# A write of an unread tile on GpSimd behind the transfers by index, in a four-layer attention and expert kernel

## The chip, the cores and the metric

The kernel runs on one core of one Trainium2 chip. The metric is the device time of one execution in microseconds; the time of a kernel is the median over its runs. Engines are named as in the profile: PE is TensorE's matmuls and PEld its weight loads, DVE is VectorE, ACT is ScalarE, POOL is GpSimd, SP is SyncE.

## What is computed

The input is `x`, 8 sequences of 256 tokens with 128 channels. Four layers follow, each added to its own input after a layer norm:

```python
x = x + _L0_attn_a_ref(_layernorm(x), w_qkv, w_proj, b_proj)     # grouped linear, 16 heads of 8
x = x + _L0_ffn_ref(_layernorm(x), router_w, router_b, w1, b1, w2, b2)
x = x + _L0_attn_b_ref(_layernorm(x), Wq, Wk, Wv, Wo, qn_w, kn_w)  # q and k normalised per head
x = x + _L0_ffn_ref(_layernorm(x), ...)                           # the same experts again
```

`_L0_ffn_ref` is a mixture of 16 experts. A softmax over `h @ router_w + router_b` gives each token a weight per expert; the four largest are kept and scaled to sum to one; the output is the weighted sum of `gelu(h @ w1[e] + b1[e]) @ w2[e] + b2[e]` over those four experts. The reference computes all experts for all tokens and multiplies by a weight that is zero for twelve of them.

## The kernel before

The kernel computes each token only in its four experts. Tokens lie 128 to a tile, 16 tiles in all, in `x_sb`; a sequence is two tiles, and the tiles fall into two halves of eight.

An expert layer `f` (0 or 1) works on a half `hf` in this way. For a group of two or four tiles the routing (`ln_route` to `rows_of`, on DVE and PE) finds for each token the rows in a DRAM buffer where copies of it go, one row in the block of each chosen expert, and puts them into `dst`. `send` (L1000) then writes the normalised rows `h` to `sent[hf]` by those indices: one transfer by index (L1007) for each tile and each of the four choices, issued by GpSimd. When all tiles of a half are sent, SyncE loads the rows of a pair of experts (`load`, L1069, into `xs`), PE transposes them (`turn`, L1085), and the two matmuls of each expert follow (`front`, L1102, and `second`, L1125); ACT's queue writes the results to `made[hf]`. `fetch` (L1254) brings them back by the indices in `src`: again one transfer by index (L1262) on GpSimd for each tile and each choice, into a tile `yg` with four buffers, or into `yg_last` for the last half of the last layer. `combine` (L1269) adds the four weighted rows to `x_sb` on DVE (L1273). The last two tiles of the last layer are not sent at all; they go through all experts in place (`all_experts`). So there are 120 sends and 120 fetches.

The first two choices of a token (`EARLY` is 2) avoid the last pair of experts, so their results can be fetched before that pair is done: `fetch` is called once for columns 0 and 1 and once for columns 2 and 3. For the first four tiles of a half, and for all six tiles of the last half, these are two separate calls:

```python
            for t in ts[:n]:
                at(end - 0.5, fetch, f, t, 0, EARLY, last)
            for t in ts[:n]:
                at(end + 1.5, fetch, f, t, EARLY, TOPK)
```

Besides the transfers by index, GpSimd sets up constants in the first 10 us, among them the four value tiles `vst` (L299: a write of 128 x 1088 f32 each), and in the first attention adds the projection's bias to `x_sb` (`add_bias`, L636; eight times). DVE adds the attention's output to the same rows later (L892).

The order of work on PE, ACT, DVE and SP is written out by hand: a list `plan` of steps with places, sorted and issued under a guard that names these four engines:

```python
    with tc.manual_schedule(engines={ET.PE, ET.Activation, ET.DVE, ET.SP}):
```

GpSimd is not named there. Its order is settled by the framework's planner when the program is built; the planner also puts in the semaphores.

Of the kernel before, what the change touches and what calls it, by code (L numbers as in the profile page):

```python
# [36 lines left out]
F32 = mybir.dt.float32  # L37
# [7 lines left out]
P = 128  # L45
# [67 lines left out]
def fast_path(  # L113
# [21 lines left out]
    nc = tc.nc  # L135
# [24 lines left out]
    def limits(cap):  # L160
        return [(E - 2) * cap] * EARLY + [E * cap] * (TOPK - EARLY)
# [6 lines left out]
    const = ctx.enter_context(tc.tile_pool(name="const", bufs=1))  # L168
# [38 lines left out]
    xf = x_in.rearrange("b n c -> (b n) c").rearrange("(t p) c -> p t c", p=P)  # L207
    of = out.rearrange("b n c -> (b n) c").rearrange("(t p) c -> p t c", p=P)
    x_sb = const.tile([P, NT, C], F32, name="x_sb")

    def load_x(b0, b1_):
        ts = slice(b0 * TB, b1_ * TB)
        nc.sync.dma_start(x_sb[:, ts, :], xf[:, ts, :])
# [104 lines left out]
    def after(ins, others):  # L318
        for o in others:
            tc.add_manual_dep(  # L320
                ins.ins,
                o.ins.name,
                mybir.DependencyInfo(mybir.DependencyClass.Sync, mybir.DependencyReason.DATA),
                reason="rows by index",
            )
# [414 lines left out]
    def needs(*what):  # L740
        assert done.issuperset(what), what
# [258 lines left out]
    def send(f, g):  # L1000

        hf = g.t0 // TPH
        needs(("rows", f, g.t0))
        before_all = list(loaded[hf] or cleared[hf])
        for i in range(g.n):
            for c in range(TOPK):
                ins = nc.gpsimd.indirect_dma_start(  # L1007
                    out=sent[hf],
                    out_offset=bass.IndirectOffsetOnAxis(
                        ap=dst[:, g.t0 + i, c : c + 1], axis=0  # L1010
                    ),
                    in_=g.h[:, i, :],
                    in_offset=None,
                )
                key = f"sent{f}{hf}"
                if scattered[hf]:
                    tc.declare_no_dep(ins.ins, group=key, reason="different rows")
                tc.add_to_no_dep_group(key, ins.ins)
                after(ins, before_all)
                scattered[hf].append(ins)  # L1020

    def plain_exp(g):
        t = work.tile([P, g.n, E], F32, tag=f"exl1{g.n}", name="ex1", bufs=1)
        nc.vector.tensor_scalar(t, g.ex, -1.0, 1.0, ALU.mult, ALU.add)
        nc.vector.reciprocal(t, t)
        nc.vector.scalar_tensor_tensor(g.ex, g.ex, 1.0, t, ALU.add, ALU.mult)
# [227 lines left out]
    def fetch(f, t, c0, c1, last=False):  # L1254

        needs(("fetchable", f, t))
        if last:
            yg[t] = many[:, t % TPH]
        elif c0 == 0:
            yg[t] = work.tile([P, TOPK, C], F32, tag="yg", name="yg", bufs=4)  # L1260
        for c in range(c0, c1):
            nc.gpsimd.indirect_dma_start(  # L1262
                out=yg[t][:, c, :],
                out_offset=None,
                in_=made[t // TPH][0 : limits(CAPS[f][t // TPH])[c]],
                in_offset=bass.IndirectOffsetOnAxis(ap=src[:, t, c : c + 1], axis=0),
            )

    def combine(t, k_next):  # L1269
        y = yg.pop(t)  # L1270
        x = x_sb[:, t, :]
        for c in range(TOPK):
            nc.vector.scalar_tensor_tensor(  # L1273
                x, y[:, c, :], wgt[:, t, c : c + 1], x, ALU.mult, ALU.add
            )
        if k_next is not None:
            ln_stats(k_next, t)
            done.add(("combined", t))
        else:
            nc.sync.dma_start(of[:, t, :], x)  # L1280
# [21 lines left out]
    def routed(f):  # L1302
        k = 2 * f + 1
        for hf in range(NH):
            earlier = []
            parts = ((0, 2), (2, 3), (3, 4)) if hf == 0 else ((0, 1), (1, 2), (2, 3), (3, 4))
            for (b0, b1_), places, fills in zip(
                parts, ROUTE[f][hf], FILL_ROUTE[f][hf], strict=True
            ):
                b0, b1_ = b0 + hf * SH, b1_ + hf * SH  # L1310
                g = Group(b0 * TB, b1_ * TB)
                g.all = (f, g.t1) == (1, NT)
                n = [base[2 * f] + b1_ * SEQ + p for p in places]
                before = list(earlier)
                at(n[0], ln_route, k, g, int(n[0]))
                at(n[1], ln_normalise, k, g, "r")
                at(n[2], ln_transpose, g, None, fills[0])
                at(n[3], route1, g)
                at(n[4], chosen, f, g)
                at(n[5], route2, g, before, in_attention(int(n[5])), fills[1])  # L1320
                if g.all:
                    at(n[7], weights_of_all, g)
                    whole.append(g)
                    continue
                at(n[6], rows_of, f, g)
                at(n[6], send, f, g)
                at(n[7], route3, f, g)
                earlier.append(g)
# [5 lines left out]
    def fetched(f, k_next):  # L1334
        k = 2 * f + 1
        for hf in range(NH):
            end = base[k] + (hf + 1) * E
            ts = [hf * TPH + i for i in range(SENT[f][hf])]
            last = k_next is None and hf == NH - 1
            n = len(ts) if last else 4  # L1340
# [4 lines that stand above are left out]
            for i, t in enumerate(ts):  # L1345
                m = COMBINE[f][hf]
                if i >= n:
                    at(end + m[i - 4], fetch, f, t, 0, TOPK)
                at(end + m[i], combine, t, k_next)
            if k_next is None:  # L1350
                continue
            for i, places in enumerate(PROJECT[hf]):
                g = gb[hf * SH + i]
                n = [end + p for p in places]
                at(n[0], to_heads, g, FILL_PROJECT[hf][i][0])
                at(n[1], project_b1, g)
                at(n[2], squares_b, k_next, g)
                at(n[3], project_b2, g, in_attention(int(n[3])))
                at(n[4], project_b3, g)
                at(n[5], project_b4, g, FILL_PROJECT[hf][i][1])  # L1360
                at(n[6], split, g, wn)
                at(n[7], stack_in, g)
# [635 lines left out]
def kernel(tc: tile.TileContext, *args):  # L1998
    nc = tc.nc
    with tc.tile_pool(name="flag", bufs=1) as pool:  # L2000
        flag = pool.tile([1, 1], I32, name="flag")
        fast_path(tc, flag, *args)
        n_bad = nc.values_load(flag[0:1, 0:1], min_val=0, max_val=6 * P)  # L2003
        with tc.If(n_bad > 0):
            general_path(tc, *args)
# [45 lines left out]
```

## Time and profile before

| what | value |
|---|---|
| median of 14 runs | 449.15 us (446.36 to 452.74) |
| the profiled execution | 451.16 us; span from first to last instruction 449.4 us |
| mean granted TensorE clock | 0.964 |
| busy: PE, ACT, DVE, POOL | 391.7, 281.0, 257.4, 245.3 us |
| sends (L1007) | 120, mean 966 ns, between 71.40 and 356.01 us |
| fetches (L1262) | 120, mean 951 and 961 ns, between 171.49 and 442.25 us |

Where the stages lie, by the timeline: the first attention runs to about 105 us, with the first half's sends from 71.4 to 111.8; the first expert layer from 116 to about 217 us, with its fetches from 171.5 to 211.5 and from 223.3 to 263.3; the second attention from about 217 to 315; its sends from 275.0 to 356.0; the second expert layer to the end, with its fetches from 372.2 to 442.3.

A line of a group reads: line of the kernel, engine, operation, output tile <- input tiles, shape, count, then busy time in us and mean ns of one, then the engine's idle time just before these instructions and what ended it. A line of a timeline reads: start and duration in us, engine, line, operation, tiles, count, and in brackets the idle time before it with what ended it; "issue" means that nothing which the profile shows was waited for.

### The profile page before, as it was taken

The numbers are of one execution on the slowest core, as the hardware profiler recorded it, in microseconds if no ns is written. First come the engines' busy times: TensorE is split into PE (matmuls) and PEld (weight loads), VectorE is DVE, ScalarE is ACT, GpSimd is POOL, SyncE is SP. The second block draws the span as 40 slices with busy tenths as digits, with TensorE's granted clock in tenths as the row PEclk, the third lists the DMA queues.
The fourth block names the chain that finished last, engine by engine and source line by source line (L and its number), as shares of the span: only waits on it lengthen the run. The fifth ranks groups of instructions, "written<-read, shape, count | busy, mean of one in ns | idle before, by whom it ended". The sixth has DMA issues, their size and how long they took to land. (4 is left out here: it accounts for less than half of the span.)

```text
span 449.4 us, 10606 instructions
## 1 busy us (share of the span) xinstructions
PE 391.7 (87%) x3884; PEld 254.1 (57%) x3884; DVE 257.4 (57%) x1037; ACT 281.0 (63%) x543; POOL 245.3 (55%) x292
## 2 busy tenths in 40 slices
PE   7999897983699999999979887888699997999991
PEld 3444553541476776766634344444477775777991
DVE  4544656564177511589648898876367413346464
ACT  4799987484453444465699988989464443553440
POOL 8110005777637725776077734777761506777772
PEclk9999998698699999999999999999699999999997
DMA  5234346751966455534434333341543334444222
GB/s 172 58 113 129 113 155 208 234 147 47 294 215 190 152 181 167 167 118 145 130 114 124 101 103 92 93 142 61 171 135 116 112 148 126 149 142 140 66 66 66
DMA packets 46668, 60.69 MB, mean 135 GB/s; under 512 B 8657, under 2 KB 28161, under 8 KB 46609
## 3 DMA queue, kind: packets, MB, share of 16 engines
q1 hardware_dynamic: 34000, 34.13, 25.4%
q0 software_dynamic: 7712, 15.81, 12.2%
q10 hardware_dynamic: 4896, 10.00, 5.8%
q8 instruction: 33, 0.54, 0.5%
q14 instruction: 27, 0.21, 0.2%
HBM read 31.86 MB, written 28.05 MB: 133 GB/s over the span
## 5 line engine op out<-in xcount | busy, mean ns | idle before, releaser
L1007 POOL DMA_INDIRECT sent<-h,dst x120 | 115.9, 966 | 79.1 <-issue 31.1
L1262 POOL DMA_INDIRECT yg<-made,src x96 | 91.3, 951 | 67.3 <-DMA made<-ys 27.2
L802 ACT ACTIVATE ex<-ps_st 128x1024 f32<-128x1024 f32 x120 | 116.1, 1027 | 14.2 <-PE ps_st L793 12.9
L1125 PE MATMUL ps_y<-w_sb,g 128*64 128x128 f32 x1216 | 80.5, 278 | 2.8 <-DVE ys L1132 2.7
L1125 PEld LDWEIGHTS ps_y<-w_sb,g 128*64 128x64 f32 x1216 | 65.1, 136 | 26.0 <-issue 11.6
L1110 ACT ACTIVATE g<-ps_h,b1T 128x320 f32<-128x320 f32 (+1 forms) x128 | 58.9, 511 | 33.1 <-PE ps_h L1102 29.7
L1102 PE MATMUL ps_h<-hs,w_sb 128*128 128x320 f32 (+1 forms) x256 | 78.9, 432 | 0.0
L1132 DVE TENSOR_TENSOR ys<-ps_y,b_bc 128x384 f32<-128x384 f32 (+1 forms) x64 | 30.3, 473 | 75.2 <-PE ps_y L1125 71.5
L823 PE MATMUL ps_av<-ex,vst 128*32 128x256 f32 x1024 | 70.5, 394 | 1.2 <-ACT av L833 0.9
L1086 ACT COPY hs<-pt_x 128x384 f32<-128x384 f32 (+1 forms) x64 | 26.1, 413 | 58.6 <-PE pt_x L1085 40.3
L1102 PEld LDWEIGHTS ps_h<-hs,w_sb 128*128 128x128 f32 x256 | 44.7, 195 | 10.3 <-issue 2.0
L793 PE MATMUL ps_st<-qst,kst 32*128 32x256 f16 x480 | 33.1, 274 | 12.2 <-ACT ex L802 7.8
L823 PEld LDWEIGHTS ps_av<-ex,vst 128*32 128x32 f32 x1024 | 27.2, 111 | 28.0 <-issue 13.6
L1085 PE MATMUL pt_x<-ident,xs 128*128 128x128 f32 x152 | 30.6, 303 | 14.1 <-DMA xs<-sent 14.1
L1273 DVE SCALAR_TENSOR_TENSOR x_sb<-yg,wgt,x_sb 128x128 f32<-128x128 f32 x96 | 33.7, 351 | 2.6
L1085 PEld LDWEIGHTS pt_x<-ident,xs 128*128 128x128 f32 x152 | 17.8, 150 | 22.0 <-issue 20.7
L636 POOL TENSOR_TENSOR x_sb<-x_sb,bp_bc 128x256 f32<-128x256 f32 x8 | 5.8, 729 | 42.5 <-DVE h L532 42.5
L793 PEld LDWEIGHTS <-kst 32*128 32x128 f16 x480 | 10.8, 92 | 30.8 <-issue 25.8
L1262 POOL DMA_INDIRECT yg_last<-made,src x24 | 23.1, 961 | 7.3 <-issue 7.0
L1198 ACT ACTIVATE g<-ps_h,b1T 128x256 f32<-128x256 f32 x32 | 13.4, 471 | 18.0 <-PE ps_h L1190 15.1
L892 DVE TENSOR_TENSOR x_sb<-pp,x_sb 128x256 f32<-128x256 f32 x16 | 6.7, 419 | 26.9 <-PE pt_h L546 15.5
L465 DVE BATCH_NORM_STATS2 st<-x_sb 128x6 f32<-128x128 f32 x64 | 17.9, 280 | 3.5 <-DMA x_sb<-in_L_attn_a_x_dram 2.4
(191 smaller groups left out, 528.7 us busy)
## 6 DMA issues: line engine op xcount, KB each, us to landing
xs<-sent SPq DMA_DIRECT2D x24, 320.0 KB
made<-ys ACTq DMA_DIRECT2D x24, 320.0 KB
sent<-zero SPq DMA_DIRECT2D x20, 256.0 KB
w_sb<-in_L_ffn_w_dram SPq DMA_DIRECT2D x16, 256.0 KB
qk_rows<-qk_parts SPq DMA_DIRECT2D x15, 256.0 KB
qst<-qk_rows SPq DMA_DIRECT2D x60, 64.0 KB
kst<-qk_rows SPq DMA_DIRECT2D x60, 64.0 KB
xs<-sent SPq DMA_DIRECT2D x8, 256.0 KB
```

The source lines that it names most:

```text
L793: nc.tensor.matmul(ps[:, hh, c * N : (c + 1) * N], kst[rows, f, c * P : (c + 1) * P], qst[rows, f, :], start=True, stop=True,)
L802: nc.scalar.activation(ex, ps.rearrange("p h (c n) -> p h c n", c=TB), AF.Exp, scale=SCALE / (UP * UP),)
L823: nc.tensor.matmul(acc[32 * i : 32 * i + 32, hf * N : (hf + 1) * N], groups[b].v[:, c, v0 : v0 + W], ex[i // 2][:, i % 2, m, :], start=(jj ...
L1007: ins = nc.gpsimd.indirect_dma_start(out=sent[hf], out_offset=bass.IndirectOffsetOnAxis(ap=dst[:, g.t0 + i, c : c + 1], axis=0), in_=g.h[: ...
L1085: nc.tensor.transpose(pt[:, (j - j0) * P : (j - j0 + 1) * P], x[:, j, :], ident)
L1086: nc.scalar.copy(hs[r][:, :, j0:j1, :], pt[:, : (j1 - j0) * P].rearrange("p (j a q) -> p a j q", a=2, q=HP),)
L1102: nc.tensor.matmul(ps[:, n, :cap], w1_sb[r][:, a, n * P : (n + 1) * P], hs[r][:, a, :RJ].rearrange("p j q -> p (j q)"), start=True, stop=True,
L1110: nc.scalar.activation(g[:, n, :RJ].rearrange("p j q -> p (j q)"), ps[:, n, :cap], AF.Gelu, bias=b1T[:, e * NI + n : e * NI + n + 1],)
L1125: nc.tensor.matmul(acc[a * HP : (a + 1) * HP, (j - j0) * C : (j - j0 + 1) * C], gs[2 * r + a][:, n, j, :], w2_sb[r][:, a, n, :], start=(n ...
L1132: nc.vector.tensor_tensor(ys[r][:, j0:j1, :], acc[:, : (j1 - j0) * C].rearrange("p (j c) -> p j c", c=C), b2_bc[:, r, :].unsqueeze(1).to_b ...
L1262: nc.gpsimd.indirect_dma_start(out=yg[t][:, c, :], out_offset=None, in_=made[t // TPH][0 : limits(CAPS[f][t // TPH])[c]], in_offset=bass.I ...
L1273: nc.vector.scalar_tensor_tensor(x, y[:, c, :], wgt[:, t, c : c + 1], x, ALU.mult, ALU.add)
```

## The change

A tile `rest_of` of 128 x 1088 f32 is added, which nothing reads, and a function `rest` that writes zeros to it on GpSimd. `send` calls it after each transfer. `fetch` calls it after each transfer of a call that was not given `last`; of the calls quoted above, the first passes `last` and the second does not.

```diff
     x_sb = const.tile([P, NT, C], F32, name="x_sb")
 
+
+    rest_of = const.tile([P, 1088], F32, name="rest_of")
+
+    def rest():
+        nc.gpsimd.memset(rest_of, 0.0)
+
     def load_x(b0, b1_):
...
                 tc.add_to_no_dep_group(key, ins.ins)
                 after(ins, before_all)
                 scattered[hf].append(ins)
+                rest()
 
     def plain_exp(g):
...
                 in_offset=bass.IndirectOffsetOnAxis(ap=src[:, t, c : c + 1], axis=0),
             )
+            if not last:
+                rest()
 
     def combine(t, k_next):
```

## The prediction

> **What bounds the kernel now.** I read the page first, for the engines' totals and their course; then the groups of GpSimd's instructions, for the price of each; then GpSimd's timeline, for the order in which they run and the holes between them; last the timeline of TensorE and the chain that ended last, for who waits on them. From the page:
>
> ```profile
> span 449.4 us, 10606 instructions
> ...
> PE 391.7 (87%) x3884; PEld 254.1 (57%) x3884; DVE 257.4 (57%) x1037; ACT 281.0 (63%) x543; POOL 245.3 (55%) x292
> ...
> POOL 8110005777637725776077734777761506777772
> ```
>
> TensorE is busiest, yet no engine bounds the whole span. GpSimd's digits show stretches at 7, and those are full: the groups and the timeline say why.
>
> ```profile
> L1007 POOL DMA_INDIRECT sent<-h,dst x120 | 115.9, 966 | 79.1 <-issue 31.1 <-DVE mb L933 13.1 <-DVE dst L988 11.7
> L1262 POOL DMA_INDIRECT yg<-made,src x96 | 91.3, 951 | 67.3 <-DMA made<-ys 27.2 <-issue 25.0 <-DMA qst<-qk_rows 11.8
> L1262 POOL DMA_INDIRECT yg_last<-made,src x24 | 23.1, 961 | 7.3 <-issue 7.0 <-POOLq L2004 0.3
> L636 POOL TENSOR_TENSOR x_sb<-x_sb,bp_bc 128x256 f32<-128x256 f32 x8 | 5.8, 729 | 42.5 <-DVE h L532 42.5
> L299 POOL MEMSET vst<- 128x1088 f32 x4 | 4.0, 996 | 0.0
> ```
>
> One transfer by index holds GpSimd for 0.96 us, and 0.30 us of "issue" stands before each. From start to start a send (L1007) takes 1.27 us (39 steps from 71.40 to 120.91), a fetch (L1262) 1.257 us (31 steps from 171.49 to 210.58, 55 from 372.22 to 441.20 at 1.254). So inside the 7s GpSimd is saturated. And others wait on it: the last send of the first half starts at 110.82, and TensorE stands still until the rows that it wrote are read back:
>
> ```profile
> 110.82 0.96 POOL L1007 DMA_INDIRECT sent<-h,dst  x1 [0.30 <-issue]
> ...
> 116.02 1.30 PE L1085 MATMUL pt_x<-ident,xs 128*128 128x128 f32 x5 [10.42 <-DMA xs<-sent]
> ```
>
> The chain that ended last is GpSimd too:
>
> ```profile
> by line: POOL yg_last L1262 0.9%; DMA yg_last<-made,src 0.6%; issue 0.4%; POOLq L2046 0.2%; DVE x_sb L1273 0.1%; DVE x_sb L1221 0.1%; DVEq L2003 0.1%; DVEq L1273 0.0%
> ```
>
> **GpSimd's account of its span.** Set-up to 10.05 us; eight bias adds (L636), 5.8; 120 sends at 1.27, 152.4; 120 fetches at 1.257, 150.8; from the end of the last fetch (442.25) to the end, 7.15. Sum 326.2. The other 123 of 449.4 us are holes: some 55 between 10 and 71.4 us (61.4 less the 5.8 of adds), and later ones of 8.6, 11.0, 11.8, 11.7, 10.3 and 16.2 us in the waits of its timeline.
>
> **What the change adds.** A write of 128x1088 f32 behind each of the 120 sends, and behind each fetch that is not called with `last`. `last` is passed only for the early two columns of the last six tiles, 12 fetches; the later two columns of the same tiles are fetched without it. So 120 + 108 = 228 writes. Nothing is removed, no transfer is added, and no other engine gets an instruction.
>
> **Price of one.** The trace has the very shape: the four writes of L299. Their records last 0.99 to 1.00 us, but from the start of one to the next instruction is 0.96. All 228 write one tile, so each may have to wait for the end of the one before. For such a pair the nearest rows are the iota at 9.65 (0.13 long) and the cast that reads it at 9.85: 0.07 us between. So one write costs 0.96 to 0.99 + 0.07 = 1.06; I take 1.00, since a write behind a transfer finds its predecessor long done and only writes in a row can pay the gap. 228 x 1.00 = 228 us (219 to 242). The page on GpSimd's records agrees that the spacing, not the record, is the price: the Trainium skill, Perfetto Trace Analysis, "GPSIMD Engine Instruction", calls the spans unreliable and has one time from start to start; by the records alone the sum would be 227, by the spacing 219.
>
> A rule speaks against the change more than these rows do: the Trainium skill, SBUF — State Buffer, "SBUF: two separate sides", has GpSimd and VectorE share a port pair under an exclusive lock, so that a VectorE operation in a two-port mode and a GpSimd instruction block each other outright. No row here shows it: the four L299 writes lie beside a VectorE that is 43% busy in the first 10 us and all last the same. If each of the 48 normalisations (L532, 0.351 us) held up one write, the rule would add 17 us; the sum goes without it.
>
> **Where the writes run.** GpSimd is not among the four engines whose order is written out by hand; its order is settled by the planner when the program is built. The timeline shows that the planner moves writes ahead of work which waits:
>
> ```profile
> 2.54 0.10 POOL L239 MEMSET rows_of_heads<- 128x16 f32 x1
> 2.58 0.99 POOL L299 MEMSET vst<- 128x1088 f32 x1
> 3.54 0.19 POOL L240 TENSOR_SCALAR_AFFINE_SELECT rows_of_heads<-rows_of_heads 128x16 f32<-128x16 f32 x1
> 3.67 0.99 POOL L299 MEMSET vst<- 128x1088 f32 x1
> 4.63 0.19 POOL L244 TENSOR_SCALAR_AFFINE_SELECT rows_of_heads<-rows_of_heads 128x16 f32<-128x16 f32 x1
> ```
>
> L299 stands far below L240 and L244 in the source and still runs between them. The new write depends on nothing but its predecessor, not on the transfer it is written behind, so I expect it not behind its transfer but pulled forward, in a block of some 55 to 65 between 10 and 71 us, and then in blocks between groups of sends and fetches, ahead of its place in the source. The first 55 us cost nothing: they lie in the hole ahead of the first send, beside attention, which does not need GpSimd. What is behind a block in GpSimd's queue is late by the block: the bias adds (VectorE's L892 needs them only some 20 us or more later), then the sends, behind them the loads `xs` on SyncE, TensorE's L1085 and the whole expert stage; then the fetches, behind them `combine` (L1273), the next attention, its routing, and the next sends. Each transfer late makes its consumer late, so the waits of GpSimd that are in the trace of before (8.6 to 16.2 us each) close up: by the time it comes there, what it waited for is done. From then on GpSimd is the bound of the whole kernel.
>
> **The sum.** So the span is GpSimd's own work and what waits are left: 326.2 + 228.0 + W. For W I take 6 us net: of the late holes the largest, 16.2 us before the first fetch of the last layer, may partly stay if the writes have run out by then, against some 20 places where a write stands just ahead of a transfer and covers its 0.30 us of issue. Bounds: W from -9 (30 places covered, no wait) to +25 (that hole whole and 9 more). 326.2 + 228.0 + 6 = 560.2 us of span. The profiled execution took 451.16 us by the clock for 449.4 of span, 1.8 more, and lies 2.0 above the median of 449.15; so the median goes to 560. Ends: 326.2 + 219 - 9 = 536; 326.2 + 242 + 25 = 593. It does not much matter where the blocks lie, as long as GpSimd never waits.
>
> **Rivals.**
> (1) The planner leaves each write behind its transfer. Then the 55 us hole and the waits for the expert stages (16.2 and about as much again) stay empty: 326.2 + 219 + 55 + 30 = 630; if each write covers the next 0.30 us of issue, 216 x 0.30 = 65 less: 565. For it: the source order. Against: the rows of L299.
> (2) Not slower: the writes cost next to nothing, since a transfer and a write overlap on GpSimd, or an unread write is dropped when the program is built. For it: at 7.14 a short write of 0.15 us starts, and at 7.20 a transfer, before the write's end. If every write cost those 0.06 us, 228 would be 14 us, all inside the holes: 449 to 452. It decides if two transfers with a write between them still start within 1.3 us. Against: long writes at 2.58 to 6.05 let nothing start before 0.96 us, and unread writes do run now; this tile has no reader and no waiter:
>
> ```profile
> L2037 POOL MEMSET const-uint8-127<- x1: 116/116/116, 0.4 to 0.4; 128x1 uint8 x1
> ```
>
> (3) Between them: the writes fill all holes and all issue time. GpSimd's idle time is 449.4 - 245.3 = 204 us, issue included; 219 to 242 us of writes leave 15 to 38 over: 465 to 490, some more with waits. It needs the planner's holes to be the chip's to the microsecond, and a write in front of every transfer.
>
> **How the numbers follow.** Blocks ahead, 0.82 (536 to 593); behind each transfer, 0.10 (565 to 630); filling everything, 0.05 (465 to 520); not slower, 0.03. The range for 8 in 10 is 533 to 598: the main case with its bounds, and the lower half of the first rival. About 0.5% (2.2 us) is what a measurement of this kernel can tell from no change: faster 0.01, same 0.02, slower 0.97.
>
> **What would show it.** Right: GpSimd's row at 9 from 10 us on, busy 245 + about 225 us; a group of 228 writes 128x1088 near 0.99 us each; the first send some microseconds after 71.4; the waits of L1007 and L1262 other than issue gone but for one or two; TensorE waiting on `xs<-sent` and VectorE on `yg` far longer than the 14.1 and 5 us of now; 120 sends and 120 fetches at the same 0.96. Wrong: writes spaced well above 1.06 us (the lock), transfers and writes strictly in turn, holes of 10 us left on GpSimd, or an unchanged step of 1.27 between transfers with writes among them.

## The result and the profile after

The changed kernel takes 576.24 us (median of 10 runs, 575.47 to 576.91), against 449.87 for the kernel before in the same comparison (47 runs): a ratio of 1.2818 (1.2784 to 1.2852). The profiled execution took 576.02 us for a span of 574.3. From its page:

```profile
span 574.3 us, 10834 instructions
...
PE 406.1 (71%) x3884; PEld 261.1 (45%) x3884; DVE 282.0 (49%) x1037; ACT 282.4 (49%) x543; POOL 473.9 (83%) x520
...
POOL 9999997789888898888988779978888798377773
```

GpSimd has 228 instructions more (520 against 292) and 228.6 us more of busy time, and its digits stand at 7 to 9 all along but for two 3s, a wait and the end. A 7 is no slack here, as before: 0.96 of every 1.26 us. Every other engine has its old number of instructions. VectorE is busier by 24.6 us, to which a later paragraph comes back, and TensorE by 14.4 us, at a mean granted clock of 0.869 instead of 0.964. The groups, and below them TensorE's line as it was before:

```profile
L215 POOL MEMSET rest_of<- 128x1088 f32 x228 | 230.0, 1009 | 11.6
L1013 POOL DMA_INDIRECT sent<-h,dst x120 | 115.3, 961 | 35.0 <-issue 33.6
...
L1269 POOL DMA_INDIRECT yg<-made,src x96 | 91.5, 954 | 38.4 <-issue 28.1
L1092 PE MATMUL pt_x<-ident,xs 128*128 128x128 f32 x152 | 32.7, 321 | 87.6 <-DMA xs<-sent 87.6
...
L1282 DVE SCALAR_TENSOR_TENSOR x_sb<-yg,wgt,x_sb 128x128 f32<-128x128 f32 x96 | 34.0, 354 | 33.7 <-DMA yg<-made,src 31.6
```

```profile
L1085 PE MATMUL pt_x<-ident,xs 128*128 128x128 f32 x152 | 30.6, 303 | 14.1 <-DMA xs<-sent 14.1
```

The transfers last as long as before. What is gone are their waits: the sends had 79.1 us of idle time ahead of them and now have 35.0, nearly all of it issue. TensorE's wait for the rows that were sent went from 14.1 to 87.6 us, VectorE's idle time ahead of L1282 from 2.6 (L1273 before) to 33.7, of which 31.6 for fetched rows. GpSimd's timeline has the order in which the writes run; the last five writes ahead of the first send, and the end of the first 24 sends:

```profile
79.53 5.28 POOL L215 MEMSET rest_of<- 128x1088 f32 x5
84.98 1.05 POOL L1013 DMA_INDIRECT sent<-h,dst  x1 [0.17 <-issue]
...
114.19 0.96 POOL L1013 DMA_INDIRECT sent<-h,dst  x1 [0.31 <-issue]
115.14 4.21 POOL L215 MEMSET rest_of<- 128x1088 f32 x4
119.51 0.96 POOL L1013 DMA_INDIRECT sent<-h,dst  x1 [0.16 <-issue]
```

66 of the 228 writes stand ahead of the first send, two of them within the set-up, the others around the bias adds: some 70 us of writes in a hole of 55. The first send comes at 84.98 instead of 71.40. Behind it follow blocks of 1 to 26 writes between groups of 4 to 24 transfers, and the last writes end at 489.02, ahead of all fetches of the last layer. Of the waits of 8.6 to 16.2 us that GpSimd had before, one is left, of 7.29 (496.31, for `made<-ys`, when the writes had run out); besides it there are idle times of 2.31 (325.67, put down to issue) and of 1.18 (517.20, for `x_sb` of L1282). TensorE's first use of the sent rows shows how the delay is handed on:

```profile
133.69 1.30 PE L1092 MATMUL pt_x<-ident,xs 128*128 128x128 f32 x5 [25.06 <-DMA xs<-sent]
```

It started at 116.02 before. The difference of 17.67 us is the late first send (13.58) and the block of four writes among the sends of this half (115.14 to 119.35).

So the 124.9 us of longer span fall into two parts: 13.58 us up to the first send, and 111.3 from there to the end, where 162 writes at 1.066 us are 173 us and the waits that closed took up some 60 of them.

### The profile page after: what moved, and what is told of

The parts are those of the page before. It is cut to its first block, busy times and chain, and to the rows that moved or that the text cites. A ratio compares the mean times of both kernels' runs of the same rounds, so it can differ in the third digit from the quotient of the medians.

```text
span 574.3 us, 10834 instructions
## 1 busy us (share of the span) xinstructions
PE 406.1 (71%) x3884; PEld 261.1 (45%) x3884; DVE 282.0 (49%) x1037; ACT 282.4 (49%) x543; POOL 473.9 (83%) x520
## 5 line engine op out<-in xcount | busy, mean ns | idle before, releaser
L215 POOL MEMSET rest_of<- 128x1088 f32 x228 | 230.0, 1009 | 11.6
L1013 POOL DMA_INDIRECT sent<-h,dst x120 | 115.3, 961 | 35.0 <-issue 33.6
L1092 PE MATMUL pt_x<-ident,xs 128*128 128x128 f32 x152 | 32.7, 321 | 87.6 <-DMA xs<-sent 87.6
L1132 PE MATMUL ps_y<-w_sb,g 128*64 128x128 f32 x1216 | 82.7, 283 | 7.4 <-DVE ys L1139 7.3
L1132 PEld LDWEIGHTS ps_y<-w_sb,g 128*64 128x64 f32 x1216 | 66.8, 139 | 31.5 <-issue 11.9
L1109 PE MATMUL ps_h<-hs,w_sb 128*128 128x320 f32 (+1 forms) x256 | 80.8, 440 | 0.0
L829 PE MATMUL ps_av<-ex,vst 128*32 128x256 f32 x1024 | 74.8, 414 | 2.4 <-ACT av L839 2.0
L1109 PEld LDWEIGHTS ps_h<-hs,w_sb 128*128 128x128 f32 x256 | 46.2, 201 | 10.7 <-issue 2.6
L1282 DVE SCALAR_TENSOR_TENSOR x_sb<-yg,wgt,x_sb 128x128 f32<-128x128 f32 x96 | 34.0, 354 | 33.7 <-DMA yg<-made,src 31.6
L555 ACT COPY hT<-pt_h 128x256 f32<-128x256 f32 (+1 forms) x30 | 11.6, 387 | 37.8 <-PE pt_h L552 28.6
L799 PEld LDWEIGHTS <-kst 32*128 32x128 f16 x480 | 10.7, 93 | 27.6 <-issue 25.3
```

The source lines that it names most:

```text
L215: nc.gpsimd.memset(rest_of, 0.0)
L799: nc.tensor.matmul(ps[:, hh, c * N : (c + 1) * N], kst[rows, f, c * P : (c + 1) * P], qst[rows, f, :], start=True, stop=True,)
L829: nc.tensor.matmul(acc[32 * i : 32 * i + 32, hf * N : (hf + 1) * N], groups[b].v[:, c, v0 : v0 + W], ex[i // 2][:, i % 2, m, :], start=(jj ...
L1013: ins = nc.gpsimd.indirect_dma_start(out=sent[hf], out_offset=bass.IndirectOffsetOnAxis(ap=dst[:, g.t0 + i, c : c + 1], axis=0), in_=g.h[: ...
L1092: nc.tensor.transpose(pt[:, (j - j0) * P : (j - j0 + 1) * P], x[:, j, :], ident)
L1109: nc.tensor.matmul(ps[:, n, :cap], w1_sb[r][:, a, n * P : (n + 1) * P], hs[r][:, a, :RJ].rearrange("p j q -> p (j q)"), start=True, stop=True,
```

## The experiments

For reading the numbers: the first eleven runs fell on chips on which the kernel before itself takes 665 to 676 us, at a granted clock of about 0.81, and only the last run on one where it takes 451.55. Ratios are to the kernel before on the same chip. The times that experiments 1, 2, 3 and 5 expected are for a kernel before at 450 us; on these chips they were not met, and they are not tested there. What the difference between these chips is became a question of its own (experiments 6 to 11); until then the readings rest on GpSimd's rows and on the stretch up to the first sends, in which the timelines agree; transfers last 0.95 to 0.97 us on all of these chips.

**1. Two tiles in turn.** Is part of a write's price the wait for the write before, which fills the same tile?

```diff
-    rest_of = const.tile([P, 1088], F32, name="rest_of")
+    rest_of = [const.tile([P, 1088], F32, name=f"rest_of{i}") for i in range(2)]
...
-        nc.gpsimd.memset(rest_of, 0.0)
+        nc.gpsimd.memset(rest_of[n_rest[0] % 2], 0.0)
+        n_rest[0] += 1
```

> The 228 writes go in turn to two tiles, so a write no longer overwrites what the write just before it wrote. Theory: GpSimd's own queue is the bound, and a write in a row costs 1.06 us from start to start only because it waits for the end of the one before; then rows of writes go back to about 0.97 us each, 228 x 0.09 = 20 us less, 553 to 558 us. Rival: the 1.06 us is the write itself or VectorE in its way; then nothing changes, 574 to 578 us, and the spacing stays 1.06.

The time, 728.53 us (ratio 1.0955, 1.0883 to 1.1027), missed what was expected, but the row in dispute is plain. The same stretch of GpSimd's timeline, first of the changed kernel, then of this one:

```profile
13.12 8.54 POOL L215 MEMSET rest_of<- 128x1088 f32 x8
```

```profile
13.20 8.56 POOL L216 MEMSET rest_of<- 128x1088 f32 x9
```

Eight writes in one, nine in the other. Over all blocks the step is 1.066 us with one tile and 0.947 with two: 0.119 us of each write in a row is the wait for the end of the one before. What the tighter row costs is seen on VectorE, in the same stretch:

```profile
18.38 6.38 DVE L540 TENSOR_SCALAR h<-x_sb,mv,rstd 128x128 f32<-128x128 f32 x2
```

In the kernel before this pair takes 0.60 us (17.75, L532), in the changed kernel 1.37 (18.25, L538). Over the whole execution the mean of the 48 normalisations is 351 ns before, 606 in the changed kernel and 1151 here (378 on such a chip without any write, in experiment 10):

```profile
L532 DVE TENSOR_SCALAR h<-x_sb,mv,rstd 128x128 f32<-128x128 f32 x48 | 14.3, 351 | 1.1 <-DMA sent<-h,dst 0.5
```

```profile
L538 DVE TENSOR_SCALAR h<-x_sb,mv,rstd 128x128 f32<-128x128 f32 x48 | 20.9, 606 | 1.1 <-DVE rstd L480 0.5
```

```profile
L540 DVE TENSOR_SCALAR h<-x_sb,mv,rstd 128x128 f32<-128x128 f32 x48 | 33.5, 1151 | 1.2 <-issue 0.2 <-DVE rstd L482 0.2
```

The pair ends at 24.76, as GpSimd's run of twelve writes does (24.60). With one tile a gap of 0.06 us stands behind each write (a step of 1.066 for a row of 1.009), with two there is none. That this is what makes the whole kernel slower than the one before is not shown.

**2. Writes behind the fetches only.** Do the writes stay where the source has them?

```diff
                 scattered[hf].append(ins)
-                rest()
```

> Writes only behind the 108 fetches, none behind a send. Theory (a write is not tied to its transfer, the planner pulls it into its own holes): the same block of some 65 writes still stands before the first send, which starts near 85 us as with all 228, all 108 writes have run before the first fetch, and the later holes of before come back; 326 + 108 x 1.06 + some 50 us of holes = 485 to 495 us. Rival (each write delays the transfer behind which it is written): the first send at 71.4 us, the sends untouched, fetches 2.2 us apart in the first layer's fetches from 171 us on; 510 to 540 us.

671.28 us (1.0004, 0.9948 to 1.006). GpSimd's timeline:

```profile
74.36 10.60 POOL L215 MEMSET rest_of<- 128x1088 f32 x10
85.13 1.05 POOL L1013 DMA_INDIRECT sent<-h,dst  x1 [0.17 <-DMA qst<-qk_rows]
```

No write belongs to a send any more, and the first send is as late as in the changed kernel (84.98). 66 writes stand ahead of it, as many as there. The planner fills the hole with whatever writes there are, from however far down in the source.

**3. Only the first 48 writes.** Are those that fit into the first hole free?

```diff
-        nc.gpsimd.memset(rest_of, 0.0)
+        n_rest[0] += 1
+        if n_rest[0] <= 48:
+            nc.gpsimd.memset(rest_of, 0.0)
```

> Only the first 48 of the 228 writes are made. Theory: they fill the hole between 10 and 71.4 us, 10 + 6 + 48 x 1.06 = 67 us, end before the first send is released, and cost nothing: the time of before within 0.5%, 448 to 452 us, first send at 71.4 us. Rival (GpSimd's writes hold up VectorE): VectorE's normalisations in the first attention are longer, 0.35 to 0.6 us, and the first attention with them; 453 to 458 us and the first send later.

662.54 us (0.9973, 0.9935 to 1.0011): no difference. All 48 ran between 9.62 and 64.47 us, and the first send came at 69.49, no later than the 71.40 of before. Some 51 us of GpSimd's work cost nothing there, though the 48 normalisations took 575 ns in the mean. On a chip where the kernel before takes 450 us this kernel was not timed.

**4. Each write bound behind its transfer** (rival 1 of the prediction, made to happen).

```diff
-    def rest():
-        nc.gpsimd.memset(rest_of, 0.0)
+    def rest(ins):
+        with tc.issue_after(ins.ins):
+            nc.gpsimd.memset(rest_of, 0.0)
```

> Every write is bound to be issued after the transfer behind which it stands in the source; same number of writes. Theory (GpSimd's work and the holes that it leaves unused): a single write between two transfers costs about 0.89 us, as the one at 251.09 us after the change did, so 326 + 228 x 0.89 + the first hole of 55 us that now stays empty + some 30 us of later holes = 605 to 620 us; the first send is back at 71.4 us and the first half's sends end near 140 us. Rival (it does not matter where the writes stand): 570 to 580 us.

617.39 us, and 614.82 in a second comparison (ratios 0.9284, 0.9226 to 0.9342, and 0.9211, 0.9142 to 0.9279). For the repeat:

> The writes bound behind their transfers, as in e4, once more, for a comparison with a kernel before at 450 us. Theory (GpSimd's account and the holes that stay empty): 605 to 620 us against 576 for the change; the first send near 71.4 us, the first half's sends done near 140 us, one write between two transfers costs 0.89 us. Rival (placement does not matter): 570 to 580 us. If the kernel before again takes some 665 us: about 617 us, as e4.

From GpSimd's timeline of the first:

```profile
102.97 0.96 POOL L1014 DMA_INDIRECT sent<-h,dst  x1 [0.16 <-issue]
103.94 1.02 POOL L216 MEMSET rest_of<- 128x1088 f32 x1
105.12 0.96 POOL L1014 DMA_INDIRECT sent<-h,dst  x1 [0.17 <-DVE x_sb L899]
```

From send to send 2.15 us: a write starts as the transfer ends, and the next transfer starts 0.16 us behind the write instead of 0.30 behind a transfer. The prediction's account of GpSimd gives 326.2 + 228 x (2.15 - 1.265) = 528, plus the hole ahead of the first send (70.59 - 15.85 = 54.7) and seven later waits (36.3): 619, and the span was 616.9. What was not foreseen is the sign: where the kernel before takes 666, more work on the engine made it faster.

**5. Writes of half the size**, placed by the planner.

```diff
-    rest_of = const.tile([P, 1088], F32, name="rest_of")
+    rest_of = const.tile([P, 544], F32, name="rest_of")
```

> The unread tile has half the columns, 544 instead of 1088; still 228 writes. Theory (GpSimd's own work is the bound): the writes of 512 columns in the set-up take 0.52 us, 0.47 from start to start, and a write in a row pays 0.10 more, so 0.47 to 0.57 us each, 107 to 130 us in all; with all holes filled 326 + 119 = 445 is below the time of before, so GpSimd is no longer the bound throughout and some of its waits stay: 326 + 119 + 15 to 40 = 460 to 485 us, less than half of the 126 us that 228 writes of 1088 columns add. Rival (each write costs by its number, not by its size): 560 to 576 us.

656.25 us (0.989, 0.9819 to 0.9962). The step in a block was 0.61 us. Between 0.61 for 544 columns and 1.066 for 1088 lies 0.84 ns a column and 0.15 us that do not depend on the size, most of it the wait for the write before (0.119 in experiment 1). The first send came at 87.64, no sooner than with full writes: shorter writes, but more of them (119 instead of 66), are put ahead.

**6. The change once more, unaltered**, on a chip where the kernel before takes 676.

> The change itself, unaltered, on the chip of the runs e1 to e5, where the kernel before takes 665 us at a granted TensorE clock of about 0.82 instead of 450 at 0.96. Theory (two bounds, whichever is later: GpSimd's account of 326 + 228 x 1.06 + 8 = 576 us, and TensorE, which on this chip alone takes 665): the writes lie in GpSimd's longer holes and cost much less than the 126 us of the first comparison, 660 to 700 us, ratio 1.00 to 1.05. Rival (the writes cost GpSimd's queue the same wherever they run): ratio near 1.19 to 1.28, 790 us or more. If the chip is as in the first comparison, 574 to 578 us.

692.4 us in the median of four runs that spread from 677.5 to 700.5, too far for an interval, against 676.16: 0 to 4% more by the single runs, where the main result is 28%. Up to the first send (85.03) its timeline is that of the changed kernel. What differs comes behind it: VectorE and ScalarE, often together, have idle times put down to "remote", that is to no instruction whose recorded end lies just before; they are called stops from here on. Those over 2.5 us on VectorE last 3 to 19 us each and sum to 160 us here and 127 in experiment 3, but to 12 and 14 us in the two runs of experiment 4, and in the traces of the kernel before and of the main result there are none. All begin beside unbroken runs of transfers by index on GpSimd and end at most some 4 us after the last transfer of the run, at times within a block of writes that follows it; none lies ahead of the first send. What was left in experiment 4 lies at, or just behind, the twelve fetches that have no write behind them. So the next three runs set the step between transfers.

**7 and 8. A short write behind every transfer**, bound as in experiment 4, with the twelve fetches that had none included; 64 columns, and 272.

```diff
-    rest_of = const.tile([P, 1088], F32, name="rest_of")
+    rest_of = const.tile([P, 64], F32, name="rest_of")
...
-            if not last:
-                rest(ins)
+            rest(ins)
```

> A write of 128x64 (a seventeenth) behind each of all 240 transfers, each bound to its transfer. By GpSimd's account: a short write of set-up takes 0.1 to 0.2 us and a transfer behind a write starts 0.16 us after it instead of 0.30, so the work of GpSimd hardly grows (0 to 15 us) and, where the kernel before takes 450, this one takes 450 to 465. On a chip where the kernel before takes some 666 us, with joint stops of VectorE, ScalarE and TensorE beside unbroken runs of transfers: if any instruction between two transfers ends these stops, sums of such stops below 20 us and 450 to 480 us; if the length of the pause matters, stops remain in part, 500 to 650; if the stops have nothing to do with transfers that follow each other, 660 to 680.

> A write of 128x272 (a quarter, some 0.27 us by a quarter of the 1.01 us row) behind each of all 240 transfers, each bound to its transfer. By GpSimd's account from 326.2: 240 x (0.27 + 0.07) less 240 x 0.14 of issue time covered = 48 us more, of which part lies in holes: 455 to 500 where the kernel before takes 450. On a chip where it takes some 666: 470 to 510 if any write between two transfers ends the joint stops of the engines; 540 to 640 if the pause of 1.06 us that the full write makes is needed; 666 and more if the stops do not depend on it.

With 64 columns 675.21 us against 673.71 (1.0018, 0.9972 to 1.0063), with 272 columns 589.06 against the same 673.71 (four runs, 581.12 to 599.92; no interval). One of the stops, of the kernel with 64 columns, as the timelines of VectorE and ScalarE and, below them, the DMA queues of a window inside it have it:

```profile
365.34 0.42 DVE L899 TENSOR_TENSOR x_sb<-pp,x_sb 128x256 f32<-128x256 f32 x1 [17.33 <-remote]
```

```profile
365.20 0.58 ACT L840 COPY av<-ps_av 128x512 f32<-128x512 f32 x1 [11.66 <-remote]
```

```profile
q0 software_dynamic: 96, 0.20, 16.1%
```

VectorE stood from 348 to 365 us; of all queues only the one that GpSimd's transfers feed moved anything from 356 to 360 us, and the stop ended some 3 us after the last transfer of the run (362.10). TensorE's rows have the `pp` that VectorE reads at 347, and hardly any work behind it:

```profile
346.80 0.61 PE L887 MATMUL pp<-wo_b,oT 128*128 128x128 f32 x4
350.44 0.61 PE L800 MATMUL ps_st<-qst,kst 32*128 32x256 f16 x4 [3.04 <-issue]
353.59 0.61 PE L800 MATMUL ps_st<-qst,kst 32*128 32x256 f16 x4 [2.53 <-issue]
366.22 0.69 PE L553 MATMUL pt_h<-ident,x_sb 128*128 128x128 f32 x2 [12.02 <-ACT qkv L665]
```

But the end of a matmul's row is not yet its signal. The trace also records the updates of semaphores: the one that TensorE's matmuls raise was updated at 352.43, then not until 365.17, and from there to 365.44 six times. ScalarE's copy started at 365.20 and VectorE's sum at 365.34. In the trace of before no update of this semaphore comes more than 1.6 us behind the recorded end of its matmul; for this `pp` it is 18 us. Every stop over 2.5 us in every run here ends with an update of this semaphore. So in a stop VectorE and ScalarE wait for TensorE, whose signals come late and then in a bunch.

An instruction between two transfers is not enough: the write of 64 columns takes just the issue time's place, and the step stays at 1.28 us.

**9. A write of 544 columns behind every transfer.**

```diff
-    rest_of = const.tile([P, 272], F32, name="rest_of")
+    rest_of = const.tile([P, 544], F32, name="rest_of")
```

> A write of 128x544 behind each of all 240 transfers, each bound to its transfer; the steps from transfer to transfer were 1.27 us with a write of 64 columns, 1.47 with 272 and 2.15 with 1088, and the joint stops of VectorE and ScalarE, where they occur, summed to some 129, 64 and 14 us. With 544 columns a step takes 0.96 + 0.16 + 0.6 = 1.72. If the stops fall with the rate of transfers: 20 to 40 us of stops, and a time of 545 to 580, below the 589 of 272 columns and the 615 of 1088. If only a pause of a whole microsecond ends them: 60 us of stops or more, 600 to 640. If the stops do not depend on the writes: 660 and more.

529.43 us against 664.69: a ratio of 0.7975 (0.7909 to 0.804), better than expected, and not one stop:

```profile
span 526.1 us, 10847 instructions
...
POOL 8100158988598829998697959889886369999994
```

The dose is clear. Steps of 1.27 us (experiments 3 and 10), 1.28, 1.47, 1.70 us gave 127 and 142, 129, 64 and 0 us of stops on VectorE, and 2.15 none where a write stood.

**10 and 11. The clears of the first send buffer earlier**, without any write; then with the writes of 544 columns. In the trace of before, the first send waits for these clears (SyncE issued the last at 66.86), while its indices are there at 59.1.

```diff
-        at(2.8 + 2 * (j - AT_ONCE), clear_rows, 0, j, NZ)
+        at(2.8 + 1.4 * (j - AT_ONCE), clear_rows, 0, j, NZ)
```

> The kernel before, without any write, with the clears of the first send buffer planned every 1.4 places instead of every 2. In the trace of before the first send (71.40) waits for the last of these clears, not for its indices, which are there at 59.1. If the clears decide: the first send some 5 to 10 us earlier, and the kernel faster by up to 8 us, at 0.985 to 0.995 of before. If the sends then only wait for indices and the first half's last send moves by under 2 us: no change, 0.997 to 1.003.

The first send came at 59.50, and the time did not change where the kernel before takes 664.69: 662.91 (0.9962, 0.9921 to 1.0004). The last send of the first half came at 122.09, and in experiment 3, with the clears as before, at 120.48: the gain was gone by then. VectorE's first stop in that trace lies between, but experiment 3 has one like it (75.21 to 92.36), so that alone does not explain it:

```profile
82.32 0.42 DVE L632 COPY vst<-pv 128x256 f32<-128x256 f32 x1 [18.88 <-remote]
```

> The two edits together: a write of 128x544 bound behind each of the 240 transfers, and the clears of the first send buffer planned every 1.4 places. With the writes alone the span was 526.1, without a joint stop, and GpSimd almost full from its first send at 71.42 us; with the clears alone the first send came at 59.50. If GpSimd's account holds: first send at 59 to 60, and the time up to 12 us below 529, 517 to 527, since holes of 10.5 and 12.3 us in waits for made<-ys may take up a part. If the stops come back because sends now lie beside other work of the first attention: 540 and more.

516.13 us, 1 us below the range that was expected, but on the one chip of the later runs where the kernel before takes 451.55: a ratio of 1.1458 (1.1374 to 1.1542) there. The first send stood at 60.74, and

```profile
L216 POOL MEMSET rest_of<- 128x544 f32 x240 | 136.4, 568 | 0.1
```

adds 240 x (1.70 - 1.265) = 104 us to GpSimd's account: 326.2 + 104.4 + 44.9 (hole up to the first send) + 41.6 (seven later waits) = 517, and the span was 514.1. Its span is 12.0 us below that of experiment 9, whose first send was 10.7 later. So with these writes one account fits both kinds of chip, though no kernel with them was run on both; without writes (450 and 665) or with writes in blocks (576 and 692) the two kinds differ. Where the kernel before takes 450 us only the change and this kernel were timed, and both are slower; the early clears alone were not timed there.

## Why the prediction was right, and where it was off

**Direction and cause: right.** The predicted span was 560.2, the measured one 574.3, and the cause is the one named: GpSimd, with 123 us of holes, got 228 writes and became the bound. Most of the predicted signs are in the profile: 120 sends and 120 fetches at the old 0.96 us, the long waits other than issue gone but for one, TensorE waiting for `xs<-sent`. GpSimd's row does not stand at 9 from 10 us on, but at 7 to 9, since the issue time ahead of most transfers stays.

**The place of the writes: right.** Pulled forward into one stretch ahead of the first send (66 against an estimate of 55 to 65) and then into blocks. Experiment 2 shows that the source line of a write does not matter, experiment 3 that those in the first hole do not delay the first send.

**The price of a write: the term that was mis-sized.** The prediction took 1.00 us, with 1.06 as the top of its range for writes in a row, and argued that a write behind a transfer finds its predecessor done. Nearly all writes stand in a row, by the prediction's own reading of the planner, so the gap was to be paid nearly every time: 1.066. Experiment 1 shows that 0.119 of it is the wait for the write before. 228 x 0.066 = 15 us is the whole miss of 14.1 us of span.

**The waits W: right, some 6 us.** Idle times of 7.3, 2.3 and 1.2 us were left, 9.9 beyond the 0.30 of issue that the account has for each transfer. Against them, each of 16 blocks that end just ahead of a transfer saves about 0.21 us (four writes move the send at 119.51 by 4.06, not by 4 x 1.066 = 4.26): 3.4. So W was 6.5, and 326.2 + 243.0 + 6.5 = 575.7 for a span of 574.3.

**The lock between GpSimd and VectorE: an effect is there, on the other side.** The prediction weighed the Trainium skill, SBUF — State Buffer, "SBUF: two separate sides", by which a GpSimd instruction and a VectorE operation in a two-port mode shut each other out; it found no row for it, and asked what it would cost the writes. The writes hardly pay: 1.009 us each, 1.019 for the 30 that lie beside a normalisation and 1.007 for the others. VectorE pays, above all in operations like the normalisation (TENSOR_SCALAR, one tensor in and one out), which went from 351 to 606 ns; L1282, with two tensor inputs, stayed at 354, and at 371 in the 22 that lie beside writes. Which mode a VectorE operation ran in no trace here shows. VectorE's busy time grew by 24.6 us in all; the account of GpSimd closes without them, so they lie off the path. Experiment 1 shows what it costs VectorE where GpSimd leaves no gap.

**The rivals.** (1) Writes strictly behind their transfers: experiment 4 has it at 617, inside the 565 to 630 given and close to the upper sum. Its lower one fails: a write covers 0.14 us of the next issue, not 0.30. Compared so, the planner's blocks saved about 42 us of span (616.9 to 574.3), but the two were not run on one kind of chip: on chips with stops the change takes 692 (experiment 6), more than these 617. (2) Not slower: the writes are there, at a full microsecond each, and hold the engine. (3) All holes and issue filled: 16 places of covered issue, not 200; 120 sends still have 33.6 us of issue ahead of them.

## What to carry to other kernels

When work is added to an engine that has no dependence on the rest, write that engine's account (own work, holes, what would be left of each hole) instead of looking at shares: at 55% busy GpSimd had room for 55 us ahead of its first send and for little behind it, because every later hole was a wait for something that its own delay pushed back. Price an instruction by its step from start to start in the order in which it will run: in a row on the same tile, in a row on two tiles in turn, and behind a transfer it was 1.066, 0.947 and 0.88 us for one and the same write (from transfer to transfer 2.15 us instead of 1.265 in the last case). And look at the neighbours, not only at the engine itself: VectorE had 24.6 us more of busy time without one instruction more.

## What was not expected of the hardware

On four of the five chips of the later runs, VectorE and ScalarE stop, often together, for 3 to 19 us while GpSimd issues transfers by index 1.27 us apart, some 130 to 160 us in all on VectorE: the kernel before takes 665 to 676 us there and 450 elsewhere. In experiment 10, which has no writes, these stops are 142 of the 211 us by which the span is longer than that of before (660.6 and 449.4); the rest is not accounted for. The stops fall to 64 us of 584 with a step of 1.47 us and are gone at 1.70, so that 240 useless writes make the kernel 20% faster there.

Each of these waits ends with a signal of TensorE that comes late. What holds the signal back stays open. The transfers themselves do not slow down (0.95 us each). One rival is untested, the recording of the profile: every run on record has a span and a granted clock, so all were recorded, and the traces from the chips with stops hold fewer of the semaphore updates that transfers make, 3,856 to 5,775 against 7,703 to 7,963 in the three traces from the other kind. That recording costs time on those chips is therefore not excluded, though experiment 9 lost as many (5,012 are left) and has no stop. Nor is it known why chips of the other kind, at the same step, show no stop.
